# Layer 0 attention: four row groups per score step, four column groups for values, a later transpose, and a different split of PSUM copies

## Chip, cores and metric

The kernel runs on one core of a Trainium2 chip. The metric is the device time of one execution in microseconds (us); lower is better. The core's engines are TensorE (PE, with its weight loads as PEld), VectorE (DVE), ScalarE (ACT), GpSimd (POOL) and SyncE (SP, which here only issues DMAs). Each engine works through its own queue in order, and the engines wait for one another by semaphores.

## What is computed

Two transformer layers with the norm after each part, in fp32, on x of shape 4 x 256 x 512. The change touches only the attention of layer 0, cut here to what matters:

```python
# D_MODEL 512, 32 heads, 8 key/value heads, HEAD_DIM 16, GROUP 4
q = (x @ Wq + bq)  # 32 heads of 16
k = (x @ Wk + bk)  # 8 heads of 16, each used by 4 query heads
v = (x @ Wv + bv)
scores = einsum('bhqd,bhkd->bhqk', q, k) / sqrt(16)
scores = where(causal, scores, -1e9)
p = softmax(scores)
out = einsum('bhqk,bhkd->bhqd', p, v)
x = layernorm(x + out @ Wo + bo)
x = layernorm(x + x @ dequantized(W).T + bias)   # layer 0's feed-forward
# layer 1: attention with 32 heads of 128 and a distance bias, a ternary feed-forward, two norms
```

## The kernel before

**Layout of layer 0's attention.** A tile is 128 tokens; a batch has two query tiles (qt = 0, 1). The 8 key/value heads of 16 channels lie on 128 partitions, two heads in each strip of 32 partitions. `kT` (a0, written at L390) holds the keys twice: copy e keeps head 2r + e of strip r and has the other zeroed (the factor `even`). So a matmul over one strip of 32 partitions with key copy e gives the scores of one head, 2r + e for strip r. `qT[:, i, :]` holds the queries of group member i. `v` holds the values of each strip's head pair in zero-padded blocks of 32 columns, so that e = 0 and e = 1 add up into one strip of 32 output partitions.

**Steps.** `run` (L323 on) goes over 64 steps `(b, qt, h, i)`: 4 batches, 2 query tiles, 2 halves of the heads, 4 group members. A step treats four heads, 128 queries and w = (qt + 1) * 128 keys, with causal cuts:

- `begin0` (L473 on): the scores. For j = 0, 1 one matmul over strip 2h + j, whose moving operand is both key copies at once (2w columns, L482). It writes a PSUM tile `sc` of 128 x 2 x 2 x 256 fp32, two banks of 2 KB; the pool `ps_s0` has two such tiles. Then DVE adds the causal mask to the diagonal block (L487) and takes the negated maximum over keys (L490); ACT computes four exponentials with their sums (L274, a helper that layer 1 uses too). DVE's reciprocal (L279) and POOL's division (L282) of the step before come last.
- `transpose0`, `lag=3` steps later: PE transposes each 128 x 128 block of the probabilities through PSUM (L297), four to a bank, and `evacuate` copies the bank to `prT` in SBUF.
- `end0`, two more steps later (`more=2`), after each fourth step: the values (L531), matmuls with 32 output columns each, into the PSUM tile `o`. The two strips of a half h go to two column groups of the array. After h = 1 the tile is copied and `tail0` is queued: output projection (L438), norm, transposes (L270), feed-forward (L455), norm, transposes for layer 1.

Between, `fill` advances the tails and `project0` of the next batch (transposes L270, keys L386, queries L399, values L414). The order that a queue finally has is chosen when the program is built, from this program order and from what is ready by estimated durations; some reciprocals and POOL operations are pinned.

**PSUM.** Eight banks: `ps_w` three (transposes, projections), `ps_s0` four (two score tiles), `ps_o0` one. **Copies.** `evacuate` (L95 to L102) alternates between DVE (L100) and ACT (L102).

```python
if not last:
    turn[0] ^= 1
if turn[0] and not last:
    nc.vector.tensor_copy(dst, src)
else:
    nc.scalar.copy(dst, src)
```

**Layer 1** starts with products of weight and token quarters (`p_k`, `p_q`, `p_v`, L632). Its scores are at L968, with a bias added by DVE at L976, and its values at L1008. Nothing of it is edited.

Of the kernel before, what the change touches and what calls it, by code (L numbers as in the profile page):

```python
# [12 lines left out]
F32 = mybir.dt.float32  # L13
# [3 lines left out]
ALU = mybir.AluOpType  # L17
AX = mybir.AxisListType
PSUM = bass.MemoryType.PSUM

P = 128
B, S, D = 4, 256, 512
NTT = B * S // P
NC = D // P
NKV, G = 8, 4
BLK = 32
ROWS = 64
EPS = 1e-5
MASKED = -3.0e38

# [19 lines left out]
def distance_table():  # L52

    rel = P + np.arange(P)[:, None] - np.arange(2 * P)[None, :]
    dist = -np.sqrt(np.maximum(rel, 0).astype(np.float32))
    return np.where(rel >= 0, dist, np.float32(MASKED)).astype(np.float32)


@with_exitstack
def block_kernel(  # L60
# [20 lines left out]
    nc = tc.nc  # L81
    slopes = [float(s) for s in alibi_slopes()]

    def pool(stack, name, bufs=1, **kw):
        return stack.enter_context(tc.tile_pool(name=name, bufs=bufs, **kw))
# [4 lines left out]
    dram = pool(ctx, "dram", 4, space=bass.MemoryType.DRAM)  # L90

    turn = [0]
    last = []

    def evacuate(dst, src):  # L95

        if not last:
            turn[0] ^= 1
        if turn[0] and not last:
            nc.vector.tensor_copy(dst, src)  # L100
        else:
            nc.scalar.copy(dst, src)  # L102
# [18 lines left out]
    la = ctx.enter_context(ExitStack())  # L121
    wa = pool(la, "wa", side="right")
    a0 = pool(la, "a0", 2, side="right")
    causal = wa.tile([P, P], F32, name="causal")
    make_causal_mask(nc, causal, MASKED)
    ps_w = pool(ctx, "ps_w", 3, space=PSUM)
    ps_s0 = pool(la, "ps_s0", 2, space=PSUM)
    ps_o0 = pool(la, "ps_o0", 1, space=PSUM)
    ring = [ps_w, "w"]

# [102 lines left out]
    def load_weights1(kv):  # L233
        wq1 = w1.tile([P, NC, G * P], F32, tag="wq1", name=f"wq1_{kv}", bufs=1)
        wo1 = w1.tile([P, G, D], F32, tag="wo1", name=f"wo1_{kv}")
        if kv % 2 == 0:
            wk1 = w1.tile([P, NC, 2 * P], F32, tag="wk1", name=f"wk1_{kv}", bufs=1)
            nc.sync.dma_start(wk1, w_qkv_v[:, :, NQ + kv * P : NQ + (kv + 2) * P])
            wk_pair[kv // 2] = wk1
        nc.sync.dma_start(wq1, w_qkv_v[:, :, ts(kv, G * P)])  # L240
        weights1[kv] = (wq1, wo1)
        if kv == 0:
            load_output_weight(kv)
# [29 lines left out]
    def exponentials(pr, sc, nm, sums, i, w):  # L273
        nc.scalar.activation(  # L274
            pr[:, i, 0:w], sc, AF.Exp, bias=nm[:, i : i + 1], accum_out=sums[:, i : i + 1]
        )
# [9 lines left out]
    def softmax_tiles(sp, name, bufs):  # L286
        nm = sp.tile([P, G], F32, tag="nm", name=f"nm_{name}", bufs=bufs + 2)
        sums = sp.tile([P, G], F32, tag="sums", name=f"sums_{name}", bufs=bufs + 2)
        pr = sp.tile([P, G, 2 * P], F32, tag="pr", name=f"pr_{name}", bufs=bufs)
        return nm, sums, pr  # L290

    def transposed_probabilities(name, pr, parts):

        for kt, dst in parts:
            pt = bank_t(f"pt_{name}_{kt}")
            for i in range(G):
                nc.tensor.transpose(pt[:, i, :], pr[:, i, ts(kt, P)], ident)  # L297
            evacuate(dst, pt.rearrange("p i (j q) -> p i j q", q=32))
# [43 lines left out]
    def advance(queue):  # L342

        while queue:
            if next(queue[0], None) is not None:
                return
            queue.popleft()

    def exhaust(queue):
        while queue:  # L350
            advance(queue)
# [82 lines left out]
    def tail0(tt, oT):  # L434

        py = bank_m(f"py_{tt}")
        for i in range(G):
            nc.tensor.matmul(py, oT[:, i, :], wop[:, i, :], start=(i == 0), stop=(i == G - 1))  # L438
        y = s0.tile([P, D], F32, tag="y", name=f"y_{tt}")
        nc.vector.tensor_tensor(y, py, x[tt], ALU.add)  # L440
        factors = norm_factors(y, f"a{tt}")
        yield True
        x1 = s0.tile([P, D], F32, tag="x1", name=f"x1_{tt}")
        normalise(x1, y, factors)
        yield True
        if tt < NTT - 1:
            yield True
            yield True
        x1T = s0.tile([P, NC, P], F32, tag="x1T", name=f"x1T_{tt}")
        transposed(x1T, x1, f"x1_{tt}")  # L450
        nc.gpsimd.tensor_tensor(x1, x1, fb_b, ALU.add)
        yield True
        pf = bank_m(f"pf_{tt}")
        for c in range(NC):
            nc.tensor.matmul(  # L455
                pf, x1T[:, c, :], wfT[:, c, :], start=(c == 0), stop=(c == NC - 1)
            )
        y2 = s0.tile([P, D], F32, tag="y", name=f"y2_{tt}")
        nc.vector.tensor_tensor(y2, pf, x1, ALU.add)
        factors = norm_factors(y2, f"b{tt}")  # L460
        yield True
        x2[tt] = xp.tile([P, D], F32, tag="x", name=f"x2_{tt}")
        normalise(x2[tt], y2, factors)
        yield True
        if tt < NTT - 1:
            yield True
            yield True
        transposed(x2T[:, :, ts(tt, P)], x2[tt], f"x2_{tt}")
        yield True

    ahead, tails = deque(), deque()

    def begin0(b, qt, h, i):  # L473

        qT, kT, _ = qkv0[b]
        w = (qt + 1) * P
        name = f"0_{b}_{qt}_{h}_{i}"
        nm, sums, pr = softmax_tiles(a0, name, 6)
        sc = ps_s0.tile([P, 2, 2, 2 * P], F32, tag="s", name=f"sc_{name}")
        for j in range(2):  # L480
            rows = slice(32 * (2 * h + j), 32 * (2 * h + j) + 32)
            nc.tensor.matmul(  # L482
                sc[:, j, :, 0:w], qT[rows, i, ts(qt, P)], kT[rows, :, 0:w], start=True, stop=True
            )
        scf = sc.rearrange("p j e k -> p (j e) k")
        diag = scf[:, :, w - P : w]
        nc.vector.tensor_tensor(  # L487
            diag, diag, causal.unsqueeze(1).to_broadcast([P, G, P]), ALU.add
        )
        nc.vector.tensor_reduce(nm, scf[:, :, 0:w], AX.X, ALU.max, negate=True)  # L490
        for n in range(G):
            exponentials(pr, scf[:, n, 0:w], nm, sums, n, w)
        divide0()
        undivided.append((pr, sums, w))
        return pr

    open0 = {}
    undivided = []

    def divide0():  # L500


        if undivided:
            divided(*undivided.pop(), True)

    def transpose0(b, qt, h, i, pr):
        name = f"0_{b}_{qt}_{h}_{i}"
        if i == 0:
            open0["p", h] = a0.tile(
                [P, 2, G, 4, 4, 32], F32, tag="prT", name=f"prT0_{b}_{qt}_{h}"  # L510
            )
        prT = open0["p", h]
        transposed_probabilities(
            name,
            pr,
            [(kt, prT[:, kt, i].rearrange("p j n q -> p n j q")) for kt in range(qt + 1)],
        )
        return prT

    def end0(b, qt, h, i, prT):  # L520
        if i < G - 1:
            return
        if h == 0:
            open0["o"] = ps_o0.tile([P, G * P], F32, tag="o", name=f"o0_{b}_{qt}")
        o = open0["o"]
        v = qkv0[b][2]
        for kt in range(qt + 1):
            for e in range(2):
                for j in range(2):
                    r = 2 * h + j  # L530
                    nc.tensor.matmul(  # L531
                        o[32 * r : 32 * r + 32, :],
                        v[:, kt, r, ts(e, 32)],
                        prT[:, kt, :, :, 2 * j + e, :],
                        start=(kt == 0 and e == 0),
                        stop=(kt == qt and e == 1),
                    )
        if h == 1:
            oT = a0.tile([P, G, P], F32, tag="oT", name=f"oT0_{b}_{qt}")
            evacuate(oT.rearrange("p i q -> p (i q)"), o)  # L540
            tails.append(tail0(2 * b + qt, oT))

    def before0(step):
        b, qt, h, i = step
        if (qt, h, i) == (0, 0, 0):
            if b == 0:
                for _ in range(3):
                    advance(ahead)
            else:
                exhaust(ahead)  # L550
            if b + 1 < B:
                ahead.append(project0(b + 1))
            if b == 1:
                load_weights1(0)

    def fill():
# [3 lines left out]
    ahead.append(project0(0))  # L560
    tails.append(feed_forward_weight())
    run(
        [(b, qt, h, i) for b in range(B) for qt in range(2) for h in range(2) for i in range(G)],
        begin0,
        transpose0,
        end0,
        before0,
        fill,
        lag=3,
        more=2,  # L570
        rest=divide0,
    )
    la.close()


# [470 lines left out]
    def fill1():  # L1046
# [16 lines left out]
        lag=1,  # L1063
# [39 lines left out]
```

## Time and profile before

| | us |
|---|---|
| median of three runs | 972.62 (970.39 to 972.8) |
| the profiled execution, its own time | 970.91 |
| its span, first to last instruction | 968.9 |
| granted clock, mean share of full speed | 0.995 |

| engine | busy us | share of the span |
|---|---|---|
| PE | 939.5 | 97% |
| PE weight loads | 556.0 | 57% |
| DVE | 619.7 | 64% |
| ACT | 316.3 | 33% |
| POOL | 445.6 | 46% |

Layer 0's attention begins with its first scores at 14 us and ends with its last exponential at 261 us; layer 1's first product starts at 280 us. In that stage the instruction groups of the edited functions are these (instructions; mean ns of one):

| group | line | instructions, mean |
|---|---|---|
| scores, 512 columns | L482 | 128, 640 |
| scores, 256 columns | L482 | 128, 426 |
| mask | L487 | 64, 692 |
| maximum, 1024 and 512 per partition | L490 | 32, 1220 and 32, 685 |
| exponentials, 256 and 128 per partition | L274 | 128, 474 and 128, 367 |
| division, 1024 and 512 per partition | L282 | 32, 1894 and 32, 1112 |

How to read it: an fp32 matmul appears as two instructions. Matmuls are pipelined and their ends are modelled, so durations of neighbours overlap; the distance from one start to the next is what a matmul costs PE. In the chain of waits a line's duration is that distance. A line of the timeline has start, duration, engine, line, what it writes and reads, how often, and in brackets the idle time of the engine before it with what ended that.

### The profile page before, as it was taken

How to read it: one execution, taken by the hardware profiler on the slowest of the kernel's cores; microseconds unless marked ns; L12 is line 12 of the kernel's file. 1: busy time of each engine (PE TensorE's matmuls, PEld its weight loads, DVE VectorE, ACT ScalarE, POOL GpSimd, SP SyncE). 2: the span in 40 equal slices, each digit the busy share in tenths (PEclk: the TensorE clock that was granted, in tenths of full speed). 3: DMA queues.
4: the chain of work that ended last, by engine and by line, in shares of the span. 5: the costliest groups of instructions: out<-in, count | busy, mean ns of one | idle time of the engine just before them, and what ended most of it. 6: DMA issues, size and time to landing. Idle time of an engine off the chain costs nothing.

```text
span 968.9 us, 11389 instructions
## 1 busy us (share of the span) xinstructions
PE 939.5 (97%) x3593; PEld 556.0 (57%) x3593; DVE 619.7 (64%) x1291; ACT 316.3 (33%) x1194; POOL 445.6 (46%) x461
## 2 busy tenths in 40 slices
PE   7999999999899999999999999999999999999996
PEld 5645555554344445566666666666666666666652
DVE  3876767777633446665666665766676666666566
ACT  2664564555511002333222222122222212224441
POOL 3463552644446213444533553444633634556732
PEclk9999999999999999999999999999999999999998
DMA  9500000000020011354443443433443334332001
GB/s 237 185 1 1 1 1 1 1 1 1 1 87 0 22 44 39 103 139 120 122 134 90 123 133 109 130 109 87 131 130 91 128 77 119 113 105 69 1 33 55
DMA packets 76418, 74.45 MB, mean 77 GB/s; under 512 B 5957, under 2 KB 52678, under 8 KB 76358
## 3 DMA queue, kind: packets, MB, share of 16 engines
q1 hardware_dynamic: 75014, 72.02, 26.1%
q10 hardware_dynamic: 1344, 1.70, 0.6%
q8 instruction: 29, 0.48, 0.2%
q14 instruction: 31, 0.25, 0.1%
HBM read 49.58 MB, written 24.12 MB: 76 GB/s over the span
## 4 chain that ended last, share of the span: by engine, by line
PE 82%; POOL 9%; DVE 5%; ACT 2%; DMA 1%; issue 1%; ACTq 0%; POOLq 0%; DVEq 0%
PE p_q L632 18%; PE po L881 14%; PE sc L968 7%; PE o L1008 7%; PE p_k L632 5%; PE p_v L632 5%; PE o L531 5%; PE sc L482 4%; PE pt L297 3%; PE pq L399 3%; PE py L438 3%; PE pf L455 3%; PE py L842 2%; POOL pr L282 2%; POOL x L903 2%; ACT pr L274 1%
## 5 line engine op out<-in xcount | busy, mean ns | idle before, releaser
L274 ACT ACTIVATE pr<-sc,nm 128x256 f32<-128x256 f32 (+1 forms) x512 | 209.4, 420 | 364.7 <-DVE nm L984 277.2
L282 POOL TENSOR_TENSOR pr<-pr,sums 128x512 f32<-128x512 f32 (+1 forms) x128 | 190.1, 1485 | 232.1 <-DVE sums L279 223.9
L976 DVE SCALAR_TENSOR_TENSOR sc<-table,sc 128x128 f32<-128x128 f32 (+1 forms) x256 | 86.0, 356 | 34.7 <-PE sc L968 32.4
L274 ACT ACTIVATION_READ_ACCUMULATOR pr<-sc,nm 128x1 f32 x512 | 103.5, 202 | 0.0
L968 PEld LDWEIGHTS sc<-kT,qT 128*128 128x128 f32 x512 | 82.3, 191 | 35.1 <-issue 29.7
L968 PE MATMUL sc<-kT,qT 128*128 128x256 f32 (+1 forms) x512 | 95.0, 327 | 0.0
L1008 PE MATMUL o<-prT,v 128*128 128x512 f32 x192 | 92.8, 592 | 0.0
L308 DVE STREAM_TRANSPOSE blocks<-pr 128x512 f32<-128x512 f32 x84 | 57.6, 698 | 45.2 <-POOL pr L282 45.2
L646 DVE TENSOR_TENSOR qT<-p_q,qT 128x512 f32<-128x512 f32 x96 | 64.6, 685 | 33.6 <-PE p_q L632 32.8
L984 DVE TENSOR_REDUCE nm<-sc 128x2 f32<-128x512 f32 (+1 forms) x128 | 69.9, 550 | 1.5
L297 PE MATMUL pt<-ident,pr 128*128 128x128 f32 x432 | 62.6, 278 | 6.0 <-POOL pr L282 5.3
L297 PEld LDWEIGHTS pt<-ident,pr 128*128 128x128 f32 x432 | 49.3, 142 | 32.5 <-issue 17.1
L490 DVE TENSOR_REDUCE nm<-sc 128x4 f32<-128x512 f32 (+1 forms) x64 | 61.0, 953 | 1.1
L482 PE MATMUL sc<-kT,qT 32*128 32x256 f32 (+1 forms) x256 | 59.9, 533 | 1.6 <-ACT pr L274 1.6
L487 DVE TENSOR_TENSOR sc<-sc,causal 128x512 f32<-128x512 f32 x64 | 44.3, 692 | 26.5 <-PE sc L482 26.2
L881 PE MATMUL po<-wo,so 128*128 128x256 f32 x224 | 58.0, 381 | 2.1 <-POOL so L612 2.1
L632 PE MATMUL p_q<-x2T,ws_q 128*128 128x512 f32 x128 | 59.8, 592 | 0.0
L102 ACT COPY o<-o 128x512 f32<-128x512 f32 x29 | 17.0, 586 | 124.9 <-PE o L1008 124.9
L632 PE MATMUL p_q<-xt,ws_q 128*128 128x512 f32 x128 | 57.7, 592 | 0.0
L881 PE MATMUL po<-wo,o 128*128 128x256 f32 x224 | 57.7, 380 | 0.0
L632 PE MATMUL p_q<-x2T,wq 128*128 128x512 f32 x128 | 57.6, 592 | 0.0
L881 PE MATMUL po<-to,so 128*128 128x256 f32 x224 | 53.3, 381 | 1.0 <-POOL so L615 1.0
(155 smaller groups left out, 1435.2 us busy)
## 6 DMA issues: line engine op xcount, KB each, us to landing
way<-blocks SPq DMA_DIRECT2D x112, 128.0 KB, 2.5
prT<-way SPq DMA_DIRECT2D x28, 512.0 KB, 3.7
wq<-in_L_attn_w_qkv_dram SPq DMA_DIRECT2D x8, 1024.0 KB, 5.3
wo<-in_L_attn_w_o_dram SPq DMA_DIRECT2D x8, 1024.0 KB, 5.4
way<-blocks SPq DMA_DIRECT2D x112, 64.0 KB, 1.8
prT<-way SPq DMA_DIRECT2D x28, 256.0 KB, 2.6
wk<-in_L_attn_w_qkv_dram SPq DMA_DIRECT2D x4, 512.0 KB, 3.7
wv<-in_L_attn_w_qkv_dram SPq DMA_DIRECT2D x2, 1024.0 KB, 6.3
```

The source lines that it names most:

```text
L274: nc.scalar.activation(pr[:, i, 0:w], sc, AF.Exp, bias=nm[:, i : i + 1], accum_out=sums[:, i : i + 1])
L282: nc.gpsimd.tensor_tensor(pr[:, :, 0:w], pr[:, :, 0:w], sums.unsqueeze(2).to_broadcast([P, G, w]), ALU.mult)
L297: nc.tensor.transpose(pt[:, i, :], pr[:, i, ts(kt, P)], ident)
L482: nc.tensor.matmul(sc[:, j, :, 0:w], qT[rows, i, ts(qt, P)], kT[rows, :, 0:w], start=True, stop=True)
L490: nc.vector.tensor_reduce(nm, scf[:, :, 0:w], AX.X, ALU.max, negate=True)
L632: nc.tensor.matmul(bank, fixed, moving, start=(c == 0), stop=(c == 1))
L646: add = lambda dst, a, b: nc.vector.tensor_tensor(dst, a, b, ALU.add)
L881: nc.tensor.matmul(bank[:, ts(n, HALF)], left[:, c, :], right[:, c, :], start=(c == 0), stop=(c == 1),)
L968: nc.tensor.matmul(sc[:, m, 0:w], qT[:, 2 * j + m, b * S + qt * P : b * S + (qt + 1) * P], kT[:, b * S : b * S + w], start=True, stop=True,)
L976: nc.vector.scalar_tensor_tensor(sc[:, m, 0:w], table[:, 2 * P - w :], slopes[kv * G + 2 * j + m], sc[:, m, 0:w], ALU.mult, ALU.add,)
L984: nc.vector.tensor_reduce(nm[:, 2 * j : 2 * j + 2], sc[:, :, 0:w], AX.X, ALU.max, negate=True)
L1008: nc.tensor.matmul(o, v1[:, 2 * b + kt, ts(kv, P)], prT[:, kt].rearrange("p j h q -> p h j q"), start=(kt == 0), stop=(kt == qt),)
```

## The change

The step's two indices change meaning: a step is now `(b, qt, e, i)`, with the key copy e in the place of the half h.

- **Scores.** A step runs four matmuls, one for each strip of 32 partitions (four row groups), with key copy e alone (w columns). They write one of two halves of a single PSUM tile `scores0` of 128 x 4 x 2 x 256 fp32; strip r has bank r, and the two halves are the two halves of each bank. Steps alternate between the halves. The pool `ps_s0` has one tile of four banks instead of two tiles of two.
- **Values.** `end0` runs four matmuls in turn for four strips (four column groups), all of the same e; the two halves e of a tile add up in `o`.
- **Transposes** come four steps after the scores (`lag=4`), and the values one step later with them.
- **Copies.** `evacuate` gives DVE one in three in layer 0, and one in two after it.

```diff
     turn = [0]
+    shares = [3]
...
         if not last:
-            turn[0] ^= 1
-        if turn[0] and not last:
+            turn[0] += 1
+        if turn[0] % shares[0] == 1 and not last:
             nc.vector.tensor_copy(dst, src)
...
-    ps_s0 = pool(la, "ps_s0", 2, space=PSUM)
+    ps_s0 = pool(la, "ps_s0", 1, space=PSUM)
...
-    def begin0(b, qt, h, i):
+    scores0 = ps_s0.tile([P, 4, 2, 2 * P], F32, name="scores0")
+    half0 = [0]
+
+    def begin0(b, qt, e, i):
...
-        sc = ps_s0.tile([P, 2, 2, 2 * P], F32, tag="s", name=f"sc_{name}")
-        for j in range(2):
-            rows = slice(32 * (2 * h + j), 32 * (2 * h + j) + 32)
+        half0[0] ^= 1
+        sc = scores0[:, :, half0[0], :]
+        for r in range(4):
+            rows = slice(32 * r, 32 * r + 32)
             nc.tensor.matmul(
-                sc[:, j, :, 0:w], qT[rows, i, ts(qt, P)], kT[rows, :, 0:w], start=True, stop=True
-            )
-        scf = sc.rearrange("p j e k -> p (j e) k")
-        diag = scf[:, :, w - P : w]
+                sc[:, r, 0:w], qT[rows, i, ts(qt, P)], kT[rows, e, 0:w], start=True, stop=True
+            )
+        diag = sc[:, :, w - P : w]
...
-        nc.vector.tensor_reduce(nm, scf[:, :, 0:w], AX.X, ALU.max, negate=True)
+        nc.vector.tensor_reduce(nm, sc[:, :, 0:w], AX.X, ALU.max, negate=True)
         for n in range(G):
-            exponentials(pr, scf[:, n, 0:w], nm, sums, n, w)
+            exponentials(pr, sc[:, n, 0:w], nm, sums, n, w)
...
-    def end0(b, qt, h, i, prT):
+    def end0(b, qt, e, i, prT):
...
         for kt in range(qt + 1):
-            for e in range(2):
-                for j in range(2):
-                    r = 2 * h + j
-                    nc.tensor.matmul(
-                        o[32 * r : 32 * r + 32, :],
-                        v[:, kt, r, ts(e, 32)],
-                        prT[:, kt, :, :, 2 * j + e, :],
-                        start=(kt == 0 and e == 0),
-                        stop=(kt == qt and e == 1),
-                    )
+            for r in range(4):
+                nc.tensor.matmul(
+                    o[32 * r : 32 * r + 32, :],
+                    v[:, kt, r, ts(e, 32)],
+                    prT[:, kt, :, :, r, :],
+                    start=(kt == 0 and e == 0),
+                    stop=(kt == qt and e == 1),
+                )
...
-        [(b, qt, h, i) for b in range(B) for qt in range(2) for h in range(2) for i in range(G)],
+        [(b, qt, e, i) for b in range(B) for qt in range(2) for e in range(2) for i in range(G)],
...
-        lag=3,
+        lag=4,
         more=2,
         rest=divide0,
     )
+    shares[0] = 2
     la.close()
```

More of the change, by code (lines that the diff above doesn't have):

```diff
@@ L471, in block_kernel @@
     ahead, tails = deque(), deque()
-    def begin0(b, qt, h, i):
+    scores0 = ps_s0.tile([P, 4, 2, 2 * P], F32, name="scores0")
+    half0 = [0]
+    def begin0(b, qt, e, i):
         qT, kT, _ = qkv0[b]
         w = (qt + 1) * P
-        name = f"0_{b}_{qt}_{h}_{i}"
+        name = f"0_{b}_{qt}_{e}_{i}"
         nm, sums, pr = softmax_tiles(a0, name, 6)
-        sc = ps_s0.tile([P, 2, 2, 2 * P], F32, tag="s", name=f"sc_{name}")
-        for j in range(2):
-            rows = slice(32 * (2 * h + j), 32 * (2 * h + j) + 32)
+        half0[0] ^= 1
+        sc = scores0[:, :, half0[0], :]
+        for r in range(4):
+            rows = slice(32 * r, 32 * r + 32)
             nc.tensor.matmul(
-                sc[:, j, :, 0:w], qT[rows, i, ts(qt, P)], kT[rows, :, 0:w], start=True, stop=True
+                sc[:, r, 0:w], qT[rows, i, ts(qt, P)], kT[rows, e, 0:w], start=True, stop=True
             )
-        scf = sc.rearrange("p j e k -> p (j e) k")
-        diag = scf[:, :, w - P : w]
+        diag = sc[:, :, w - P : w]
         nc.vector.tensor_tensor(
@@ L504, in divide0, with transpose0 @@
             divided(*undivided.pop(), True)
-    def transpose0(b, qt, h, i, pr):
-        name = f"0_{b}_{qt}_{h}_{i}"
+    def transpose0(b, qt, e, i, pr):
+        name = f"0_{b}_{qt}_{e}_{i}"
         if i == 0:
-            open0["p", h] = a0.tile(
-                [P, 2, G, 4, 4, 32], F32, tag="prT", name=f"prT0_{b}_{qt}_{h}"
+            open0["p", e] = a0.tile(
+                [P, 2, G, 4, 4, 32], F32, tag="prT", name=f"prT0_{b}_{qt}_{e}"
             )
-        prT = open0["p", h]
+        prT = open0["p", e]
         transposed_probabilities(
@@ L518, in transpose0 @@
         return prT
-    def end0(b, qt, h, i, prT):
+    def end0(b, qt, e, i, prT):
         if i < G - 1:
             return
-        if h == 0:
+        if e == 0:
             open0["o"] = ps_o0.tile([P, G * P], F32, tag="o", name=f"o0_{b}_{qt}")
@@ L527, in end0 @@
         for kt in range(qt + 1):
-            for e in range(2):
-                for j in range(2):
-                    r = 2 * h + j
-                    nc.tensor.matmul(
-                        o[32 * r : 32 * r + 32, :],
-                        v[:, kt, r, ts(e, 32)],
-                        prT[:, kt, :, :, 2 * j + e, :],
-                        start=(kt == 0 and e == 0),
-                        stop=(kt == qt and e == 1),
-                    )
-        if h == 1:
+            for r in range(4):
[6 more added lines that the diff above has]
+                )
+        if e == 1:
             oT = a0.tile([P, G, P], F32, tag="oT", name=f"oT0_{b}_{qt}")
@@ L543, in before0 @@
     def before0(step):
-        b, qt, h, i = step
-        if (qt, h, i) == (0, 0, 0):
+        b, qt, e, i = step
+        if (qt, e, i) == (0, 0, 0):
             if b == 0:
```

## The prediction

> **What bounds the kernel now.** I read the page first (busy shares, the chain), then the busy time by stretch, then layer 0's instructions in order of time, step by step. The busy times by stretch, with columns PE, weight loads, VectorE (DVE), ScalarE (ACT), GpSimd (POOL), clock, DMA share and GB/s:
>
> ```profile
> 14.00:262.00 248.00, 240.76 (x1185) 130.19 (x1186) 184.47 (x350) 142.66 (x573) 119.70 (x92) 0.99 0.10 27
> 280.00:969.00 689.00, 673.63 (x2317) 412.42 (x2315) 427.92 (x924) 169.16 (x614) 318.76 (x354) 1.00 0.33 93
> ```
>
> Layer 0's attention fills 14 to 262 us. PE is busy for 240.8 of its 248 us, DVE for 184.5 and ACT for 142.7. So PE bounds this stage, with DVE next at 74%. Nothing after 280 us is edited. The chain of waits is almost unbroken PE there, and shows what the two edited groups cost:
>
> ```profile
> 120.29 1.06 PE sc L482 x4
> ...
> 206.76 0.63 PE sc L482 x4
> ...
> 214.33 3.58 PE o L531 x16
> ```
>
> A step's scores take 1.06 us of PE where two key tiles are in view (qt = 1) and 0.63 where one is (qt = 0). Sixteen value matmuls take 3.58. Each fp32 matmul is two instructions here. Now one step in order of time (start, duration, engine, line):
>
> ```profile
> 166.28 1.13 PE L482 MATMUL sc<-kT,qT 32*128 32x512 f32 x4
> ...
> 167.46 0.70 DVE L487 TENSOR_TENSOR sc<-sc,causal 128x512 f32<-128x512 f32 x1 [0.38 <-PE sc L482]
> ...
> 168.19 1.22 DVE L490 TENSOR_REDUCE nm<-sc 128x4 f32<-128x1024 f32 x1
> ...
> 169.51 0.47 ACT L274 ACTIVATE pr<-sc,nm 128x256 f32<-128x256 f32 x1 [0.83 <-DVE sums L279]
> 169.64 1.04 POOL L282 TENSOR_TENSOR pr<-pr,sums 128x512 f32<-128x512 f32 x1 [2.91 <-DVE sums L279]
> 169.76 0.30 PEld L482 LDWEIGHTS sc<-kT,qT 32*128 32x128 f32 x4 [0.84 <-issue]
> 169.77 1.13 PE L482 MATMUL sc<-kT,qT 32*128 32x512 f32 x4
> ...
> 171.23 0.22 ACT L274 ACTIVATION_READ_ACCUMULATOR pr<-sc,nm 128x1 f32 x1
> ```
>
> Scores, mask, maximum, four exponentials: strictly one after another, 166.28 to 171.45, 5.17 us. Yet the next step's scores start at 169.77, while this step's exponentials still read: two score buffers let steps overlap. That overlap is what I price below.
>
> **What the Trainium skill says.** "TensorE: Matmul & The Clock Gate", Part 3, gives four row groups (K=32, N=512) a measured 3.07x, with starts some 4 ns apart. The trace agrees for two: the pair at 154.973 and 154.980 starts 7 ns apart. No run shown has four. "TensorEngine Tiling (Array Packing)", Gotcha 1, says different row tiles may not write the same PSUM bank at once; so four groups need four banks, which the changed tile (128 x 4 x 2 x 256 fp32, 2 KB per group) gives. "PSUM — Partial Sum Buffer", "PSUM bank collisions raise a hardware error", says two engines must be kept off one bank and partition quadrant at once, whatever columns they touch. The kernel before obeys. In layer 1, two score matmuls share a bank, and DVE, idle, wants the columns of the first:
>
> ```profile
> 506.19 0.38 PE L968 MATMUL sc<-kT,qT 128*128 128x128 f32 x2
> ...
> 506.19 0.61 PE L968 MATMUL sc<-kT,qT 128*128 128x128 f32 x4
> ...
> 506.83 0.29 DVE L976 SCALAR_TENSOR_TENSOR sc<-table,sc 128x128 f32<-128x128 f32 x1 [1.47 <-PE sc L968]
> ```
>
> (The first line is the timeline cut after the first matmul's two instructions, the second after all four.) The first matmul's two instructions end at 506.57, all four at 506.79; DVE starts at 506.83. It waited for the bank, not for its columns.
>
> **The change, part by part.**
>
> *Scores on PE.* Before, two groups with 2w columns each; after, four with w. A pass of 512 columns takes 0.43 (sixteen value matmuls, two at a time: 8 x 0.43 + 0.2 = 3.6), so a step falls from 1.06 to 0.63 at qt = 1 and from 0.63 to 0.41 at qt = 0: 32 x 0.43 + 32 x 0.22 = 20.8 us less, if the four start together. Weight loads double (256 to 512); loads of different groups overlap (four in 0.30 us), and at worst add 0.1 a step, which I leave to the waits below.
>
> *Values on PE.* 192 instructions, two column groups at a time, 96 x 0.43 = 41.3; four at a time, 48 x 0.43 = 20.6. Another 20.6 us less. PE's other work in the stage stays at about 150 us (248 less 58 of scores and 41 of values, start to start), so PE would need 150 + 20.6 + 33.6 = 204 us.
>
> *The score buffers.* Here the change costs. The two halves of the new tile are the two halves of the same four banks, so every step uses all four banks. By the bank wait above, a step's group r can start only when the exponential of the step before in bank r is done, and the mask needs all four. Two buffers become one. A step then turns round in: for qt = 1, 5.17, less 0.43 of scores, plus 0.05 from last exponential to next scores (the end at 245.42 and start at 245.47 show that) = 4.79; for qt = 0, the like step at 73.77 ends at 77.62, 3.85, its least is 3.77, so 3.79 less 0.22 plus 0.05 = 3.62. Sum: 32 x 4.79 + 32 x 3.62 = 269 us. Before, the 64 steps took from 14.1 (first scores) to 261.4 (last exponential), 247.3 us, 3.86 each. The ring alone costs 269 - 247 = 22 us, more than PE's own bound, and nothing hides it, as scores, mask, maximum and exponentials are its links.
>
> *Waits in the ring.* In the steps of before, from scores to last exponential took 4.75 us on average against a least 3.77 (qt = 0), and 5.91 against 5.17 (qt = 1): 0.86 a step of waiting for DVE and ACT to finish something else. It cost little, as two buffers absorbed it. Now it is on the path. DVE and ACT are less loaded per us over a longer stage, which argues for less; PE adds a wait of its own, as scores that come ready find PE inside another matmul. Between 0 and 0.86 + 0.2 I take 0.5: 32 us. Ends: 0 and 68.
>
> *The split score group.* Exponentials end 0.45 (qt = 1) or 0.35 (qt = 0) apart, so groups 0 to 3 come ready one by one, and PE either waits with a group open or puts other work between. Behind a waiting score matmul everything on PE's queue stands: transposes, projections, values. A single group costs what the pair at 79.54 did: 0.62 to the next start for 256 columns, against 0.63 for all four together. I price it under the rivals; PE has 269 - 204 = 65 us of room for it.
>
> *PSUM copies.* 121 in the stage, 61 on DVE at 0.68 and 60 on ACT at 0.59. A third on DVE: 20 move, DVE loses 14 us and ACT gains 12. Both are links of the ring, so neither sets the end alone; that is within the 0.5. In layer 1 every second copy is DVE's as before.
>
> *Transposes four steps behind.* One more pass of the loop, no instruction more, and no DMA is moved. The six probability buffers cover a lag of four. The division on POOL waits for nothing new. Zero, and if that cover fails, one POOL division (1.9 us) per stall.
>
> *The end of the layer.* From the last exponential (261.4) to layer 1's first product (280.03) passed 18.6 us, since PE had values and feed-forward of the tiles before still to do. With PE no longer behind: reciprocal 0.2, division 1.9, transposes 1.1, copy 0.7, values 1.9, copy 0.75, output product 3.5 = 10.1. That gives back 8.5.
>
> *Sum.* Steps 269 + 32 = 301, from 14.1 to 315.1, where it was 261.4: +53.7, less 8.5 = +45. The profiled execution took 970.9, so 1016; the median of the runs is 1.7 above it (972.6), so **1017 us**.
>
> **Rivals.**
>
> *B: split groups make PE the bound (slower still).* If PE puts other work between all four groups: 32 x 4 x 0.62 + 32 x 4 x 0.41 = 132 us of scores instead of 33.6, PE at 150 + 20.6 + 132 = 303, and with 32 of waits 335 instead of 247: +88 - 8.5, 1052. For it: the step at 79.54 was already split so. Against: once group 0 has run, the others come ready within a matmul's time.
>
> *C: the halves are independent (faster).* If a step's scores may be written to one half while the other is read, two steps overlap as before and PE stays the bound with 41.4 us less: 972.6 - 41.4 + 5 of DVE waits (DVE at 171 of 207 us) = 936. Its place is the score wait at line 482; it decides as soon as the pace falls below the 3.86 us a step of before plus the 0.13 that the end gives back. For it: the columns don't overlap. Against: the layer-1 wait above, and the skill's page.
>
> *D: four groups don't overlap beyond two (the change doesn't do what it says).* Then scores keep 1.06 and 0.63 and the ring grows by 20.8: 1038. Against: the pairs 7 ns apart. It lies inside the range.
>
> **Chances.** The forecast, a ring with waits: 0.66. B: 0.14. D: 0.06. C: 0.11. Waits and savings cancel within 0.3% (about what a measurement of this kernel can tell from no change): 0.03. So slower 0.66 + 0.14 + 0.06 = 0.86, same 0.03, faster 0.11. The range starts at the ring with no waits, 1017 - 32 = 985, set at 984, and reaches to 1054, where the full waits (1053) and B's centre (1052) lie. Outside are C, the no-change case and the upper part of B.
>
> **What would show it.** Right: score matmuls (line 482) waiting for ACT in nearly every step; score starts 4.0 to 5.5 us apart; PE busy in the stage down to some 70 to 85%; values 16 in about 1.9 us; the first layer-1 product near 325; layer 1 of the same length (689 us). Wrong: scores that start while the exponentials of the step before still run in the same banks; then C holds. If groups of one step stand apart with other matmuls between and PE is above 95% busy, B.

## The result and the profile after

| | us |
|---|---|
| changed kernel, median of four runs | 1096.08 (1093.11 to 1098.44) |
| kernel before, beside it | 971.5 |
| ratio | 1.128 (95% interval 1.125 to 1.132) |
| profiled execution: own time, span | 1093.11, 1091.3 |

The change costs 125 us. The sign was forecast; the size was not (1017, range to 1054).

First the busy time by stretch, with the columns as before. Layer 1 has the same length to the microsecond, 689 us; the whole loss lies ahead of it.

```profile
14.00:389.00 375.00, 256.51 (x1449) 150.79 (x1448) 178.27 (x331) 155.91 (x594) 119.39 (x93) 0.80 0.06 17
403.00:1092.00 689.00, 673.07 (x2316) 412.19 (x2314) 427.46 (x924) 168.93 (x614) 318.23 (x354) 0.99 0.33 93
```

The stage took 375 us where it took 248. PE is busy for 256.5 of them, 68%, and its mean granted clock, the third column from the end, fell from 0.99 to 0.80. No engine is full, so the stage is bound by a chain of waits. The page's slices show the same (tenths of 40 slices; the first 14 are layer 0's attention). They also show that the mean clock is lower there than in layer 1:

```profile
PE   6867767867665689999999999999999999999996
...
PEclk9877978996766789999999999999999999999998
```

The chain of waits now goes round in the same circle in most steps (start, duration, what):

```profile
187.44 1.97 PE pt L300 x8
189.40 1.21 PE scores L489 x8
190.69 0.71 DVE scores L493
191.43 1.22 DVE nm L496
192.91 1.90 POOL pr L285
194.85 1.09 PE pt L300 x8
195.94 0.48 PE scores L489 x8
```

Scores, mask, maximum, and then not the exponentials but POOL's division and PE's transposes, and after those the next scores. One such step in order of time:

```profile
182.44 0.71 PE L489 MATMUL scores<-kT,qT 32*128 32x256 f32 x8
...
183.28 0.70 DVE L493 TENSOR_TENSOR scores<-scores,causal 128x512 f32<-128x512 f32 x1 [0.48 <-PE scores L489]
184.01 1.23 DVE L496 TENSOR_REDUCE nm<-scores 128x4 f32<-128x1024 f32 x1
185.15 0.17 DVE L282 RECIPROCAL sums<-sums 128x4 f32<-128x4 f32 x1
...
185.49 1.89 POOL L285 TENSOR_TENSOR pr<-pr,sums 128x1024 f32<-128x1024 f32 x1 [4.13 <-DVE sums L282]
...
187.07 0.21 ACT L277 ACTIVATION_READ_ACCUMULATOR pr<-scores,nm 128x1 f32 x1
187.43 1.57 PEld L300 LDWEIGHTS pt<-ident,pr 128*128 128x128 f32 x8 [4.68 <-POOL pr L285]
187.44 1.97 PE L300 MATMUL pt<-ident,pr 128*128 128x128 f32 x8 [4.29 <-POOL pr L285]
...
189.33 1.24 PE L489 MATMUL scores<-kT,qT 32*128 32x256 f32 x8
```

The four row groups work: eight instructions take 0.71 us (the starts of the four groups lie 6 to 8 ns apart in all 64 steps). The last exponential ends at 187.28, so the next scores could start at 187.33. They start at 189.33, because transposes stand ahead of them on PE's queue. Those wait for POOL's division, which waits for the reciprocal, which is pinned behind this step's maximum (185.15). After 4.29 us without work PE runs slower: the same eight transposes take 1.97 where they took 1.09 at 181.42, and the scores 1.24 where they took 0.71. The busy time by stretch shows why, if the stretches are cut where the clock can change. In this trace the granted clock has only the two values 1.00 and 0.50, and in this stage it changes only on a grid of 3.41 us:

```profile
180.39:183.80 3.41, 1.96 (x20) 1.17 (x16) 1.21 (x2) 1.46 (x5) 0.97 (x1) 1.00 0.01 2
183.80:187.22 3.42, 0.00 (x0) 0.00 (x0) 1.49 (x3) 1.87 (x8) 1.73 (x1) 1.00 0.00 0
187.22:190.63 3.41, 3.19 (x17) 2.21 (x18) 0.69 (x1) 0.65 (x2) 0.16 (x1) 0.50 0.00 0
190.63:194.04 3.41, 1.45 (x12) 1.21 (x12) 2.58 (x4) 2.37 (x8) 2.41 (x2) 1.00 0.00 0
```

PE is idle in the second stretch, and the third, with the transposes and the scores, runs at half clock. So a mean clock of 0.80 is a mix of stretches at full and at half clock.

The order in which PE's queue was built shows whose transposes these are. In the kernel before, the transposes of a step stand behind the scores of the third step after it, nearly without exception. In the changed kernel, with `lag=4` in program order, they stand 1.4 steps behind on average, 1 in most of layer 0:

```
scores            step n+1
pt                step n      (waits for POOL's division of step n)
scores            step n+2
pt                step n+1
scores            step n+3
```

The links of a step, from the timeline, means over the 32 steps of each kind in us (wait is from the end of the last exponential of the step before to this step's scores; pace is the sum of the row):

| | wait | scores | to mask | mask | to max | max | to exp | exponentials | pace |
|---|---|---|---|---|---|---|---|---|---|
| before, qt = 0 | -1.20 | 0.78 | 0.37 | 0.69 | 0.57 | 0.68 | 0.15 | 1.51 | 3.54 |
| before, qt = 1 | -1.77 | 1.13 | 0.54 | 0.69 | 0.21 | 1.22 | 0.18 | 1.94 | 4.15 |
| after, qt = 0 | 0.76 | 0.59 | 0.28 | 0.70 | 0.11 | 0.69 | 0.14 | 1.50 | 4.76 |
| after, qt = 1 | 1.39 | 0.99 | 0.45 | 0.70 | 0.14 | 1.22 | 0.17 | 1.93 | 7.00 |

Before, the wait is negative: on average the next scores began 1.2 to 1.8 us ahead of the end of the exponentials. After, it is positive in every row.

### The profile page after: what moved, and what is told of

It reads as the page before. It is cut to its first block, busy times and chain, and to the rows that moved or that the text cites. A ratio compares the mean times of both kernels' runs of the same rounds, so it can differ in the third digit from the quotient of the medians.

```text
span 1091.3 us, 11992 instructions
## 1 busy us (share of the span) xinstructions
PE 951.4 (87%) x3849; PEld 576.5 (53%) x3849; DVE 611.9 (56%) x1269; ACT 329.9 (30%) x1216; POOL 443.6 (41%) x461
## 4 chain that ended last, share of the span: by engine, by line
PE 70%; POOL 14%; DVE 11%; issue 3%; ACT 1%; DMA 1%; POOLq 0%; DVEq 0%; ACTq 0%
PE p_q L637 16%; PE po L886 12%; POOL pr L285 7%; PE sc L973 6%; PE o L1013 6%; PE pt L300 5%; PE p_k L637 4%; PE p_v L637 4%; DVE nm L496 4%; PE scores L489 3%; PE py L441 3%; PE pf L458 2%; DVE scores L493 2%; PE pq L402 2%; PE py L847 2%
## 5 line engine op out<-in xcount | busy, mean ns | idle before, releaser
L277 ACT ACTIVATE pr<-sc,nm 128x128 f32<-128x128 f32 (+1 forms) x256 | 104.8, 418 | 291.3 <-DVE nm L989 277.2
L300 PE MATMUL pt<-ident,pr 128*128 128x128 f32 x432 | 79.8, 331 | 102.3 <-POOL pr L285 101.5
L277 ACT ACTIVATE pr<-scores,nm 128x128 f32<-128x128 f32 (+1 forms) x256 | 104.1, 419 | 140.5 <-DVE sums L282 122.4
L300 PEld LDWEIGHTS pt<-ident,pr 128*128 128x128 f32 x432 | 60.5, 169 | 138.1 <-POOL pr L285 129.6
L493 DVE TENSOR_TENSOR scores<-scores,causal 128x512 f32<-128x512 f32 x64 | 44.6, 696 | 99.2 <-PE scores L489 90.7
L105 ACT COPY prT<-pt 128x512 f32<-128x512 f32 x76 | 43.9, 588 | 69.8 <-PE pt L300 69.6
L496 DVE TENSOR_REDUCE nm<-scores 128x4 f32<-128x512 f32 (+1 forms) x64 | 61.2, 956 | 1.7
L489 PE MATMUL scores<-kT,qT 32*128 32x128 f32 (+1 forms) x512 | 50.5, 472 | 5.9 <-ACT pr L277 5.8
```

Source lines behind the costliest of these rows:

```text
L277: nc.scalar.activation(pr[:, i, 0:w], sc, AF.Exp, bias=nm[:, i : i + 1], accum_out=sums[:, i : i + 1])
L489: nc.tensor.matmul(sc[:, r, 0:w], qT[rows, i, ts(qt, P)], kT[rows, e, 0:w], start=True, stop=True)
L493: nc.vector.tensor_tensor(diag, diag, causal.unsqueeze(1).to_broadcast([P, G, P]), ALU.add)
L496: nc.vector.tensor_reduce(nm, sc[:, :, 0:w], AX.X, ALU.max, negate=True)
```

## The experiments

My theory after the result (Q): the single set of banks makes the steps a ring, as forecast; and idle PE lets the transposes move forward on its queue, so that POOL's division and the transposes join the ring. Rivals: the single set alone with larger waits (S), the four-group matmuls themselves (M), the halves after all giving some overlap, the lag or the copies.

**Pinned transposes.** The transposes are queued behind the newest score matmul (`scored[0]`), which holds them four steps behind on PE's queue.

```diff
+        with tc.issue_after(scored[0].ins):
             transposed_probabilities(
```

> The changed kernel with one thing pinned: on PE's queue the transposes of a step come behind the scores of the step four later, where program order has them (in the changed kernel they stand 1.4 steps behind on average, ahead of the next scores). Theory Q (the place of the transposes on PE's queue draws the POOL division and the transposes into the ring): the wait from last exponential to next scores falls from 0.74 and 1.39 us a step (qt = 0, 1) to under 0.3, PE's clock rises, and the time falls to 1010 to 1040. Rival S (the single bank set alone costs it all): no change, above 1080.

Measured: 1054.65 us, ratio 1.086 (1.084 to 1.088). The wait ahead of the scores fell to 0.30 and 0.25 (median 0.05), as Q says, and PE now waits for the exponentials, not for POOL:

```profile
181.98 0.19 ACT L277 ACTIVATION_READ_ACCUMULATOR pr<-scores,nm 128x1 f32 x1
...
183.00 0.21 ACT L277 ACTIVATION_READ_ACCUMULATOR pr<-scores,nm 128x1 f32 x1
183.27 0.31 PEld L490 LDWEIGHTS scores<-kT,qT 32*128 32x128 f32 x8 [2.87 <-ACT pr L277]
183.27 0.50 PE L490 MATMUL scores<-kT,qT 32*128 32x128 f32 x8 [2.63 <-ACT pr L277]
183.70 0.86 PEld L300 LDWEIGHTS pt<-ident,pr 128*128 128x128 f32 x8
183.70 1.09 PE L300 MATMUL pt<-ident,pr 128*128 128x128 f32 x8
```

So the queue's order costs 41 us. But the time stayed above the 1010 to 1040 that I expected: 83 us of loss remain with the order mended, and the clock did not recover (0.83 in the stage).

**One score buffer in the kernel before.**

```diff
-    ps_s0 = pool(la, "ps_s0", 2, space=PSUM)
+    ps_s0 = pool(la, "ps_s0", 1, space=PSUM)
```

> The kernel before with one score tile of two banks in place of two tiles, nothing else of the change: two row groups, two column groups, transposes three steps behind, every second copy on VectorE. Theory Q: the loss of the second buffer brings it all; transposes move forward to 1.2 steps behind, and the steps turn round as in the changed kernel plus 0.33 us of longer scores: 1100 to 1130. Rival M (the four-group matmuls themselves are what is slow): 970 to 1000.

Measured: 1140.55 us, ratio 1.174 (1.172 to 1.176). None of the four-group matmuls is in it, and it is slower than the changed kernel. That is above the 1100 to 1130 that I expected. M falls. With the second buffer gone the transposes stand 1.2 steps behind, and this brings more than the whole of the loss; the other parts of the change together give back some 44 us of it.

**One half only.**

```diff
-        half0[0] ^= 1
```

> The changed kernel with every step writing the same half of the score tile. If the halves share the waits of their banks, they give no overlap: same as the changed kernel, 1090 to 1102. If they give some overlap: slower than 1110.

Measured: 1094.06 us, ratio 1.126 (1.124 to 1.129), against 1.128 of the changed kernel. Alternating the halves gives no overlap at all.

**No division on POOL.** The reciprocals stay; the multiplication by them is left out.

> The changed kernel without POOL's division of layer 0's probabilities (the reciprocals stay; the probabilities are left undivided, so that part of the computation is left out). Theory Q: the 1.0 to 1.9 us of the division leave the ring, the transposes stay in it: 1035 to 1065, and below 1096 by 30 at least. Rival S: no change, above 1080.

Measured: 1057.03 us, ratio 1.088 (1.086 to 1.091). The wait ahead of the scores fell to 0.40 and 0.68. S as the whole account falls: POOL, with 119 busy us of 375, was in the ring. The run changes the queue's order too: with no division to wait for, the transposes stand 0.55 steps behind on average, so the 39 us are not those of the division alone.

**Lag three, half of the copies.** `lag=3`, `shares = [2]`.

> The changed kernel with the two small parts undone: transposes three steps behind in program order, VectorE every second copy. If the queue's order follows readiness and the ring is what counts: within 1% of the changed kernel, 1085 to 1107. If the lag or ScalarE's copies are what is slow: under 1070.

Measured: 1104.92 us, ratio 1.137 (1.135 to 1.140). The transposes stand 1.2 steps behind on the queue. Undoing the two small parts makes the kernel 9 us slower, so they are not what is slow. Which of the two helps was not tried alone.

**Early reciprocal.**

```diff
-        divide0()
         undivided.append((pr, sums, w))
+        divide0()
...
-            divided(*undivided.pop(), True)
+            divided(*undivided.pop())
```

> The changed kernel with each step's reciprocal queued on VectorE right behind its own maximum, ahead of the next step's mask, in place of behind the next step's maximum; nothing else. Theory Q: POOL's division then starts with the end of the exponentials and runs beside the next scores, mask and maximum, so that the transposes no longer wait for it: 1045 to 1070. Rival S (POOL and the transposes are not in the ring): 1090 or more.

Measured: 1111.53 us, ratio 1.144 (1.142 to 1.146): a miss, slower than the changed kernel. POOL's division did start at once after the exponentials, and the wait ahead of the scores fell to 0.45 and 0.53. But the waiting moved to VectorE and ScalarE:

```profile
182.85 0.18 DVE L282 RECIPROCAL sums<-sums 128x4 f32<-128x4 f32 x1 [3.97 <-ACT pr L277]
183.65 0.70 DVE L493 TENSOR_TENSOR scores<-scores,causal 128x512 f32<-128x512 f32 x1 [0.62 <-PE scores L489]
185.84 0.69 DVE L103 COPY prT<-pt 128x512 f32<-128x512 f32 x1 [1.49 <-PE pt L300]
186.44 1.21 DVE L496 TENSOR_REDUCE nm<-scores 128x4 f32<-128x1024 f32 x1
```

The copy of the transposed block stands between mask and maximum on VectorE's queue. It waits for the transposes, these for the division, and the maximum waits behind it for 2 us. From mask to maximum and from maximum to exponentials took 0.77 and 0.89 us at qt = 1, where the changed kernel has 0.14 and 0.17. Shortening one link did not help while the transposes stayed near (1.25 steps behind). Which of the two it is, their place or the reciprocal that now holds VectorE's queue until the exponentials end (the first line), no run separates.

**Pinned, transposes twice.** PE does each probability transpose of layer 0 two times; the second writes the same values.

> The kernel with pinned transposes, with every probability transpose of layer 0 run twice (about 42 us more of PE work, behind the scores, beside the mask and maximum). If PE's low granted clock is part of the loss: the clock rises, the scores' own time falls from 0.56 and 0.97 to about 0.5 and 0.75, and the time stays or falls, 1030 to 1056. If the clock doesn't matter: slower, 1058 to 1090.

Measured: 1034.5 us, ratio 1.065 (1.063 to 1.067), 20 us less than with half of these transposes. More work on PE made the kernel faster. The stage of the pinned kernel and of this one:

```profile
14.00:352.00 338.00, 243.70 (x1452) 149.62 (x1452) 175.10 (x329) 153.54 (x591) 118.09 (x92) 0.83 0.07 20
```

```profile
14.00:327.00 313.00, 256.60 (x1796) 173.35 (x1788) 176.47 (x329) 151.97 (x591) 117.89 (x92) 0.93 0.07 21
```

The granted clock rose from 0.83 to 0.93, and the scores' own time fell from 0.56 and 0.97 to 0.51 and 0.79. So PE's lower clock, in stretches in which it has little to do, is a part of the loss. Score matmuls alone make 32 x (0.05 + 0.18) = 7 us of the 25 by which the steps got shorter; the rest is in the waits behind other PE work. The transposes stand at the same places on PE's queue in both kernels; a share of other changes of order was not separated.

**One buffer, transposes pinned.** The kernel before with one score tile, its transposes held three steps behind, as they were.

> The kernel before with one score tile and with the transposes pinned three steps behind the scores on PE's queue, as in the kernel before; two row groups, two column groups. So the queue's order is that of before and only the second score buffer is missing. If the missing buffer alone costs: a ring of 269 + 21 = 290 us plus the 50 to 70 of waits that the pinned kernel kept, last exponential near 355 to 375, time 1060 to 1085. If the loss came from the queue's order alone: under 1000.

Measured: 1097.16 us, ratio 1.128 (1.126 to 1.131). More than expected, but the rival (under 1000) is out by far: with the transposes where they were before, losing the second buffer alone costs 125 us, part of it by the clock (0.85 in the stage). Against the pinned kernel, which has the rest of the change, it is 42.5 us slower. My ring of 290 us took too little for PE: it is busy for 294 of 379 us here, and the scores stood behind it for 0.85 and 0.70 us a step.

**No norm.** The pinned kernel with doubled transposes, without layer 0's norms for seven of eight tiles.

```diff
-        normalise(x1, y, factors)
+        if tt == NTT - 1:
+            normalise(x1, y, factors)
+        else:
+            nc.gpsimd.tensor_copy(x1, y)
```

The norm's factors are left out for these tiles too, and the second norm is treated alike.

> The kernel with pinned, doubled transposes, without layer 0's norms for seven of the eight token tiles (a copy on POOL stands in their place, so that part of the computation is left out). If the waits still in the ring are the mask standing behind the norm chain on VectorE's queue: the wait ahead of the mask falls from 0.23 and 0.28 to under 0.15, the 64 steps fall from 313.5 to 280 to 300 us, and the time to 1000 to 1022. If they come from elsewhere: 1028 or more.

Measured: 1021.91 us, ratio 1.052 (1.049 to 1.055). The wait ahead of the mask fell to 0.14 and 0.12, and the 64 steps to 301 us. In the pinned kernel with doubled transposes 11 steps had a mask that stood over 0.3 us behind the tail's norm (10) or a copy (1) on VectorE's queue; here one has, behind a reciprocal.

**Values alone.** The kernel before, with the values of both halves h run together over four column groups.

```diff
+        open0["done", h] = prT
         if h == 0:
-            open0["o"] = ps_o0.tile([P, G * P], F32, tag="o", name=f"o0_{b}_{qt}")
+            return
...
-                for j in range(2):
-                    r = 2 * h + j
+                for r in range(4):
...
-                        prT[:, kt, :, :, 2 * j + e, :],
+                        open0["done", r // 2][:, kt, :, :, 2 * (r % 2) + e, :],
```

> The kernel before with the second part alone: the values of both halves h run together, four column groups in turn (after the second half; three prT buffers, and five probability buffers and one oT buffer to make room). Scores, two score tiles, lag three and copies stay as before. If four column groups halve the values' time on a PE that bounds the stage: 20.6 us less, 947 to 956. If column groups don't overlap four wide (rival M): 968 to 978.

Measured: 957.86 us, ratio 0.987 (0.985 to 0.989), just outside the 947 to 956 that I expected. This beats both kernels. In its chain of waits:

```profile
52.94 1.85 PE o L531 x16
68.70 0.97 PE o L531 x2
83.17 3.60 PE o L531 x30
```

Sixteen instructions in 1.85 us, where the kernel before had sixteen in 3.58: column groups do run four wide. Of the 20.6 us 13.6 arrived. The second line shows one loss: on PE's queue the first value matmul of seven of eight tiles stands alone, ahead of the rest. From start to start the values take 31.3 us of PE in all, 48.4 before.

**Values and copies.** The same with one PSUM copy in three on VectorE in layer 0.

> The kernel before with four column groups for the values (as in values_only) and with VectorE making one PSUM copy in three in layer 0. PE bounds the stage with two score buffers, and VectorE's waits cost little: within 5 us of values_only, 952 to 962. If ScalarE's copies delay the exponentials: over 965.

Measured: 964.29 us, ratio 0.993 (0.991 to 0.995): 6 us slower than values alone, just outside the 5 that I allowed. With two buffers, ScalarE's extra copies stand ahead of exponentials (0.38 us from maximum to exponential at qt = 1, against 0.19). So with PE as the bound this part hurts; the run with lag three and half of the copies, which undid two parts at once, cannot say whether it helps in the ring.

**Values together.** Values alone, with a tile's value matmuls held together on PE's queue (`tc.issue_after` the newest transpose).

> The kernel before with four column groups for the values, as in values_only, and with a tile's value matmuls held together on PE's queue behind the newest transposes. In values_only the first value matmul of seven of eight tiles stood alone, ahead of the others, and took 0.97 us of PE by itself: the values took 31.3 us of PE in place of the 20.6 priced (48.4 before). If these lone matmuls are where the missing 7 us went: 3 to 7 us less than values_only, 951 to 955. If not: 956 to 961.

Measured: 962.48 us, ratio 0.991 (0.989 to 0.993): a miss, not faster than values alone. The values fell to 23.5 us of PE, but other gaps opened. PE's waits with the values together, and then with values alone (engine and line, waited for: us in total, times, longest):

```profile
PE pt L298 <- POOL pr L283: 9.4, 5, 3.3
PE sc L483 <- ACT pr L275: 3.5, 7, 0.7
```

```profile
PE pt L297 <- POOL pr L282: 3.9, 3, 2.6
PE sc L482 <- ACT pr L274: 1.4, 4, 0.4
```

So holding the values together does not bring the missing 7 us. It looks as if the lone matmuls had filled gaps in which PE waits anyway: as PE is relieved, POOL's division and the exponentials begin to end its waits.

## Why the prediction was right in direction and wrong in size

- **PE bounds the stage before; layer 1 is not touched:** right. Layer 1 took 689 us in both, and values alone gained as PE was relieved.
- **Scores and values on PE:** right. 0.43 to 0.48 us (qt = 0) and 0.64 to 0.69 (qt = 1) to the next start at full clock, against 0.41 and 0.63; sixteen values in 1.85 (values alone), against 1.9. Rival D falls.
- **Two buffers become one:** right. One half gives the same time as two, and in all 64 steps the scores began at or after the end of the exponentials. Rival C falls.
- **The ring's own price of 269 us:** close. In the run without norms some 20 of the 64 steps turned round in 3.70 us (qt = 0) and 4.87 (qt = 1), the quickest there are, against 3.62 and 4.79; 64 such steps would take 274. (For qt = 0 the sum takes 3.79 where 3.77 had been read; this is 0.6 us in all.)
- **The wait bank by bank:** wrong in part. In all 64 steps of the changed kernel only the fourth exponential raises a semaphore, so bank 0, free after the first (182.17 in the pinned kernel's lines), waits with the rest until 183.27. Whether the wait belongs to the banks or to the one tile that both halves lie in, no run separates, and the lines of layer 1 leave the same question open.
- **Waits in the ring: this term was mis-sized.** I put it at 0.5 us a step, 32 us, with 68 as the upper end. It measured 375 - 269 = 106. The runs split it, each kernel having one thing more than the one above it, by the length of the 64 steps:

| kernel | 64 steps, us | less | time, us |
|---|---|---|---|
| changed | 375.4 | | 1096.1 |
| transposes pinned | 338.7 | 36.7 queue order | 1054.7 |
| and run twice | 313.5 | 25.2 with the clock | 1034.5 |
| and without norms | 301.4 | 12.1 norm chain | 1021.9 |
| ring as priced | 269 | 32 left | |

- The shares hold for this order of removal; another order could divide them otherwise. What is left, 32 us, is the size that I gave the whole term. The step that failed is "Transposes four steps behind. One more pass of the loop, no instruction more ... The division on POOL waits for nothing new. Zero". I took `lag=4` for the order on PE's queue. With two buffers the transposes stood three steps behind; with one, where nothing pinned them, they stood 1.2 to 1.4 behind, mostly ahead of the next scores, and brought in POOL's 1.9 us and their own 1.1 to 2.0. That they move because PE is idle in the build's estimate fits these orders, but was not shown. I had even named the price (one POOL division per stall), but only for probability buffers that run out.
- The clock was no step at all. I noted PE at 70 to 85% busy as a sign, and it came to 68%, but I priced its matmuls at full clock. The runs showed 0.80 in the stage, and the doubled transposes won back 25.2 us.
- So the direction was right for the reason given, but the ring alone, at 269 to 274 us in place of 247, explains only 22 to 27 of the 125 us.
- **The end of the layer:** 18.6 us from the last exponential to layer 1 became 402.5 - 388.7 = 13.8; 4.8 given back, not 8.5.
- **Rival B** gave a higher time for another reason. The four groups never stood apart, as one exponential releases them all, and PE was far from full.

The sum closes: the steps are 128.1 us longer (375.4 - 247.3), they start 0.9 earlier, and 4.8 come back at the end; 122.4, and the profiled executions differ by 1093.1 - 970.9 = 122.2.

## What to carry to other kernels

A buffer that alternated between halves of the same PSUM banks was one buffer here: before adding concurrency to the matmuls of a stage, count the banks, and price the loop that a lost buffer closes, with every link at its measured time. Then read the order on the engines' queues, not the loop's lag: where an engine becomes idle, a build that orders queues by readiness may move later work forward, and whatever that waits for joins the loop. When PE stops being the bound, do not price its matmuls at the clock that it had when it was full; look at how its work falls into short stretches.

## What the runs showed of the hardware

- PE's mean granted clock in this stage was 0.99 at 97% busy (kernel before), 0.93 at 82% (transposes twice), 0.80 at 68% (changed kernel). It is a mix of 1.00 and 0.50 on a grid of 3.41 us, and what a stretch gets goes with PE's busy share in the one before. In this stage of all the runs, 901 stretches were at full clock: where PE was busy for less than 42% of them, all 131 were followed by half clock; at 60% or more, none of 678 were. Of 349 at half clock, full clock followed 1 of 153 with PE under 80% busy, and 135 of 148 at 95% or more. So the clock fell below about half and came back only from nearly full, and a long gap was not needed: without norms no gap of PE exceeded 3.2 us, yet some 34 of the 301 us ran at half clock.
- The same eight transposes took 1.09 or 1.97 us, the same score group 0.71 or 1.24. Adding some 42 us of PE work, estimated from the 384 transposes at 0.11 us from start to start, saved 20 us.
- Four fp32 row groups start 7 ns apart. Eight instructions of 256 columns take 0.71 us in all and of 128 columns 0.50, where two groups took 1.13 and 0.70 for twice the columns each.
